# Tying the transposes and theta products of a sparse graph chunk behind the gathered products of the next chunk

## The chip, the cores and the metric

The kernel runs on one core of one Trainium2 chip. The metric is device time in microseconds (us) of one launch.

## The reference

Two graph layers with a residual and a layernorm each, on x of 8 batches, 2048 nodes, 128 features, and one adjacency matrix of 2048 x 2048 that is sparse (about 0.4% of its elements, and its diagonal, are not zero). All numbers are float32.

```python
# layer 0
res = si[:, :, None] + sj[:, None, :] + adj[None] * w_r + g_b    # si, sj: x @ parts of g_w
x = layernorm(x + einsum('bij,bjd->bid', res, x) @ weight + bias)
# layer 1: Chebyshev hops with adj, two orders (A1 and A2 are both adj)
x1 = einsum('bnf,nw->bwf', x, adj);  x2 = 2 * einsum('bnf,nw->bwf', x1, adj) - x
x = layernorm(x + relu(concat([x, x1, x2, x1, x2]) @ Theta1 + bias))
```

## The kernel before

Nodes are cut into 16 chunks of 128 rows; one row of a node holds all 8 batches (1024 numbers, 4 KB). The kernel runs in four stages.

1. To about 150 us: adj is read, masked by blocks and transposed, and each chunk is multiplied by the weight of layer 0 (Y, written to DRAM as `y0_d`). Lists of the rows that each chunk needs are made from the masks.
2. Layer 0, chunks 0 to 3, dense: all 16 blocks of a chunk are multiplied (L758).
3. Layer 0, the 12 sparse chunks, in the order of `seq`: 9 to 14, 4 to 8, 15. This is the loop that the change touches.
4. Layer 1 in two hops, `hop(1, u_d)` and `hop(2, y_d)`, over all 16 chunks. By reordering the sums, hop 1 gathers rows of `u_d`, which is the normalized x of layer 0 times a part of theta; hop 2 gathers rows of what hop 1 wrote.

A sparse chunk takes 7 gathers of 128 rows from DRAM. `gather` (L629) issues them as indirect DMAs on GpSimd (POOL) into nine buffers that are used in turn, G. All gathers of the kernel form one chain in a fixed order. Between the seven gathers of rows for a chunk, three small gathers fetch adjacency weights for later chunks into `stage` (in layer 0 and the first chunks of hop 1); `keep_r` (L657, L663, VectorE) multiplies these by a mask and puts them into `rct` (for layer 0) and `rc` (for layer 1), which hold the stationary operands.

For one sparse chunk c the loop of stage 3 issues, in program order:

- `fetch_own`, `load_x`: loads for the next chunk, on the SP queue. `put(c)`: the last of the masked weights of c.
- `own_rows` (L819): 2 products with the chunk's own rows. `listed_rows` (L837): 4 gathered blocks with 32 weight columns each, in 8 products; 2 blocks with 64 columns, in 4; 1 block with 128 columns, in 2. These 16 products are tied to each other by `in_order`.
- `make_u(*pending)`, for the chunk before c: two times `transpose4` (L182, 4 transposes each, and one copy out of PSUM, the first on VectorE at L174, the second on ScalarE at L176), then for each half 4 products with theta (L388) and a copy on ScalarE (L391), then the write of u to `u_d` on ScalarE's DMA queue (L392).
- `finish0`: two additions to x on VectorE (L371), and `layernorm`: sum (L205), mean (L208), subtraction (L209), two squares on ScalarE (L213) with their sums on VectorE (L214), square root on ScalarE (L215), reciprocal (L217), product (L218). Its result is the z that `make_u` transposes one chunk later.

After the loop, `make_u` runs once more, for chunk 15. Then hop 1 begins: `begin` for its first three chunks computes products of the transposed x with theta (L876) and with the chunk's own rows of `u_d` (L819), and the gathers from `u_d` follow, which need all of u written.

The engines' queues are not in program order: a scheduler places each instruction by the data that it needs and its own costs. Two helpers hold it: `behind` makes one instruction follow another on its engine without a semaphore, and `in_order` keeps a list of products and ties each new one behind the last. What is not tied is free to move.

```python
def in_order(mm):
    if mms:
        behind(mm, mms[-1])
    mms.append(mm)
```

Before the change, `make_u` is not tied. The scheduler puts two of the eight transposes of most chunks ahead of the products with 64 weight columns, the other six behind the last product, and the theta products between the two own-row products of the next chunk. At the end of the layer, it puts the L876 and L819 products of hop 1's first two chunks ahead of the transposes of chunk 15.

Of the kernel before, what the change touches and what calls it, by code (L numbers as in the profile page):

```python
# [18 lines left out]
def kernel(  # L19
# [29 lines left out]
    nc = tc.nc  # L49
# [4 lines left out]
    HB = B // 2  # L54
# [49 lines left out]
    def rows4(name):  # L104
        return w4.tile([P, B, D], F32, name=name, tag="w4")

    def flat(t):
        return t.rearrange("p b f -> p (b f)")


    ident = const.tile([P, P], F32)
# [59 lines left out]
    def evict(dst, src, dve=None):  # L171
        flip[0] ^= 1
        if flip[0] if dve is None else dve:
            nc.vector.tensor_copy(dst, src)  # L174
        else:
            nc.scalar.copy(dst, src)  # L176

    def transpose4(srcs, name, t=None, dve=None):

        pt = p_tr.tile([P, 4, P], F32, name=f"pt_{name}", tag="pt")  # L180
        for i, s in enumerate(srcs):
            nc.tensor.transpose(pt[:, i, :], s, ident)  # L182
        if t is None:
            t = trp.tile([P, 4, P], F32, name=f"tr_{name}", tag="tr")
        evict(t, pt, dve)
        return t
# [33 lines left out]
    def load_x(c, name, q, t=None):  # L220
        if t is None:
            t = rows4(f"{name}{c}")
        tc.keep_in_program_order(
            q.dma_start(out=t, in_=x[:, c * P:(c + 1) * P, :].rearrange("b p f -> p b f"))
        )
        return t
# [128 lines left out]
    def acc_pair():  # L355
        par[0] ^= 1
        return bank[2 * par[0]:2 * par[0] + 2]
# [9 lines left out]
    def finish0(c, accs, xr, norm=True):  # L367

        for h in range(2):
            hs = slice(h * HB, (h + 1) * HB)  # L370
            nc.vector.tensor_add(xr[:, hs, :], accs[h], xr[:, hs, :])  # L371
        if norm:
            layernorm(xr, f"0_{c}")
        return xr

    def make_u(c, z, xt, u=None):

        for h in range(2):
            transpose4([z[:, h * HB + i, :] for i in range(4)], f"p{c}_{h}",
                       xt[:, h * HB:(h + 1) * HB, :])  # L380
        if c < ND:
            nc.scalar.dma_start(out=xt_d[c], in_=flat(xt))
        if u is None:
            u = rows4(f"u{c}")
        for h in range(2):
            pp = p_sm.tile([P, HB, D], F32, name=f"pp{c}_{h}", tag="sm")
            for i in range(HB):
                nc.tensor.matmul(  # L388
                    pp[:, i, :], xt[:, h * HB + i, :], th[:, 0, :], start=True, stop=True
                )  # L390
            nc.scalar.copy(u[:, h * HB:(h + 1) * HB, :], pp)  # L391
        nc.scalar.dma_start(out=u_d[c * P:(c + 1) * P, :], in_=flat(u))  # L392

# [303 lines left out]
    def put(c):  # L697

        while jobs and jobs[0][0] == c:
            gathers(1)  # L700
        while any(w[0] == c for w in waiting):
            keep_r(*waiting.pop(0))

    pending, accs, xr = None, acc0, load_x(0, "xr", nc.sync)
    at1, ar2 = first_at[1], None
    for c in range(ND):
# [15 lines left out]
        else:  # L722
            z = finish0(c, accs, xr, c > 2)
        if c + 1 < ND:
            accs1, sit = acc_pair(), si_t(c + 1)
            at2 = first_at.get(c + 2)
            for j in range(NC):
                if c == 0:
# [7 lines left out]
                    if j == 14:  # L736
                        chunk_ranks()
                        z = finish0(c, accs, xr, False)
# [18 lines left out]
                for h in range(2):  # L757
                    mm = nc.tensor.matmul(  # L758
                        accs1[h], at1[:, j, :], Y[j][:, h * HB:(h + 1) * HB, :],
                        start=(j == 0), stop=False, skip_group_check=True,  # L760
                    )
# [4 lines left out]
        if pending is not None:  # L766
            make_u(*pending)
        z1 = z
        pending, xr = (c, z, rows4(f"xt{c}")), xr1

    def fetch(src, name, out=None):
        t = rows4(name) if out is None else out
        tc.keep_in_program_order(nc.sync.dma_start(out=flat(t), in_=src))
        return t
# [21 lines left out]
    def fetch_own(i, src, c):  # L796
        t = held.get((i, c))
        if t is None:
            t = fetch(src[c * P:(c + 1) * P, :], f"own{i}_{c}", Y[NG4 + turn[0] % 3])
            turn[0] += 1  # L800
        r = small.tile([P, P], F32, name=f"rd{i}_{c}", tag="rd", bufs=3)
        tc.keep_in_program_order(nc.sync.dma_start(
            out=r, in_=rr_d[c - ND][c * P:(c + 1) * P, 0, :] if i == 0
            else adj[c * P:(c + 1) * P, c * P:(c + 1) * P],
        ))
        own[i, c] = t, r
# [9 lines left out]
    def own_rows(i, c, accs, start):  # L816
        t, r = own.pop((i, c))
        for h in range(2):
            in_order(nc.tensor.matmul(  # L819
                accs[h], r, t[:, h * HB:(h + 1) * HB, :], start=start, stop=False,  # L820
                skip_group_check=True,
            ))
# [21 lines left out]
    with nc.allow_non_contiguous_dma(reason="512-byte rows of a diagonal block"):  # L844
        fetch_own(0, y0_d, seq[0])
        xr = load_x(seq[0], "xs", nc.sync)
        for c, c1 in zip(seq, seq[1:] + [None]):
            if c1 is not None:
                fetch_own(0, y0_d, c1)
                xr1 = load_x(c1, "xs", nc.sync)  # L850
            put(c)
            while jobs[0][0] == c1:
                gathers(1)
            accs = acc_pair()
            own_rows(0, c, accs, True)
            listed_rows(0, y0_d, c, accs)
            make_u(*pending)
            z = finish0(c, accs, xr)
            pending, xr = (c, z, x1t[c], held.get((1, c))), xr1
        for c in hops[:2]:  # L860
            fetch_own(1, u_d, c)
        for c in range(ND):
            fetch(xt_d[c], f"xt_{c}", x1t[c])
        make_u(*pending)

        def hop(i, src):
            def begin(n):
                c = hops[n]
                if (i, c) not in own:
                    fetch_own(i, src, c)  # L870
                accs = acc_pair() if n % 3 < 2 else [
                    p_sm.tile([P, HB, D], F32, name=f"acc{i}_{c}_{h}", tag="sm") for h in range(2)
                ]
                for h in range(2):
                    for b in range(HB):
                        in_order(nc.tensor.matmul(  # L876
                            accs[h][:, b, :], x1t[c][:, h * HB + b, :], th[:, i, :],
                            start=(b == 0), stop=False, skip_group_check=True,
                        ))
                own_rows(i, c, accs, False)  # L880
                return accs

            def end(c, accs):
                z = held.get((i + 1, c)) if i == 1 else None
                if z is None:
                    z = rows4(f"z{i}_{c}")
                for h in range(2):
                    hs = slice(h * HB, (h + 1) * HB)
                    if i == 1:
                        evict(z[:, hs, :], accs[h], h == 1)  # L890
                        continue
                    pt = p_tr.tile([P, HB, P], F32, name=f"pt_r{c}_{h}", tag="pt")
                    for b in range(HB):
                        in_order(nc.tensor.transpose(pt[:, b, :], x1t[c][:, h * HB + b, :], ident))  # L894
                    nc.vector.tensor_add(z[:, hs, :], accs[h], b1bc.to_broadcast([P, HB, D]))  # L895
                    nc.vector.scalar_tensor_tensor(  # L896
                        z[:, hs, :], z[:, hs, :], 0.0, pt, op0=ALU.max, op1=ALU.add
                    )
                if i == 1:
                    nc.scalar.dma_start(out=y_d[c * P:(c + 1) * P, :], in_=flat(z))  # L900
                else:
                    layernorm(z, f"1_{c}")
                    nc.scalar.dma_start(
                        out=out[:, c * P:(c + 1) * P, :].rearrange("b p f -> p b f"), in_=z
                    )

            early = [begin(n) for n in range(3)]
            for n, c in enumerate(hops):
                if i == 1 and c == 0:
                    while waiting:  # L910
                        keep_r(*waiting.pop(0))
                listed_rows(i, src, c, early[n])
                if i == 1 and n < 10:
                    gathers(3)
                if 1 <= n < NC - 2:
                    early.append(begin(n + 2))
                end(c, early[n])

        hop(1, u_d)
        hop(2, y_d)  # L920
# [21 lines left out]
    with tc.If(many == 1), nc.allow_non_contiguous_dma(reason="512-byte rows of a block"):  # L942
        for c in range(NC):
# [3 lines left out]
            z = finish0(c, accs, xr)  # L947
            nc.scalar.dma_start(out=x1_d[c * P:(c + 1) * P, :], in_=flat(z))
            make_u(c, z, rows4(f"xtd{c}"))
        for i, src in ((1, u_d), (2, y_d)):  # L950
            for c in range(NC):
                x1 = fetch(x1_d[c * P:(c + 1) * P, :], f"x1_{i}_{c}")
                xt = batches_t(x1, f"q{i}_{c}", True)
# [7 lines left out]
                z = rows4(f"zd{i}_{c}")  # L961
# [47 lines left out]
```

## Time and profile before

| | |
|---|---|
| median of 4 runs | 878.43 us (877.85 to 878.69) |
| the profiled execution | 878.73 us |
| its span, first to last instruction | 876.9 us |
| PE busy | 768.1 us (88%) |
| DVE, ACT, POOL busy | 405.8, 175.4, 437.0 us |
| TensorE clock granted, mean over the span | 0.967 |
| HBM, read and written | 345 GB/s over the span |

The profiled execution is 0.3 us above the median, and 1.8 us of it lie outside the span. In the lines of the profile, PE is TensorE's products and PEld its loads of stationary operands, DVE is VectorE, ACT is ScalarE, POOL is GpSimd, SP is SyncE; ACTq and SPq are the sequencers of these engines as they issue DMAs. A group or a line in order of time begins with its start and its length in us; the brackets at its end give the idle time of the engine ahead of it and what ended that. An idle engine is a cost only if it is the one that others wait for. float32 products with 128 moving columns appear as two passes each in the trace, products with 512 columns too, so counts of the trace are twice those of the code. Transposes appear once.

### The profile page before, as it was taken

The page shows a single profiled execution, that of the slowest core. Times are in us where ns is not written, and L with a number is a line of the kernel's source. Part 1 is how long each engine was busy: PE and PEld are TensorE (multiplying, and loading weights), DVE is VectorE, ACT ScalarE, POOL GpSimd, SP SyncE. Part 2 cuts the span into 40 slices and gives each one's busy share as a digit, 9 for nine tenths or more (in the row PEclk, how much of TensorE's full clock was granted, in tenths as well). Part 3 has the DMA queues.
Part 4 walks back from the last instruction along what each step waited for, and adds up shares of the span by engine and source line. Part 5 has one row for each costly group of instructions (what it writes and reads, how often), then busy time and mean ns, then how long its engine had stood idle before and what let it go on. Part 6 is the DMA issues. An engine that isn't in the chain of part 4 may idle for free. (4 is left out here: it accounts for less than half of the span.)

```text
span 876.9 us, 10299 instructions
## 1 busy us (share of the span) xinstructions
PE 768.1 (88%) x3607; PEld 377.1 (43%) x3607; DVE 405.8 (46%) x639; ACT 175.4 (20%) x397; POOL 437.0 (50%) x431
## 2 busy tenths in 40 slices
PE   5999999999996878979887788898999899999992
PEld 4666664465443333424335132333443334555541
DVE  5555674355984256555643000000100066677775
ACT  3655652011111112221212000000000011111111
POOL 0000000015667777777711777777653576566650
PEclk9999999899999899999989899999999999999997
DMA  8699999893386999999974899999997899999992
GB/s 281 200 311 311 300 297 294 261 364 107 79 344 183 371 344 334 345 359 367 358 306 151 283 309 333 343 326 352 372 386 278 312 321 361 341 352 358 352 351 95
DMA packets 171416, 265.05 MB, mean 302 GB/s; under 512 B 17069, under 2 KB 122069, under 8 KB 169180
## 3 DMA queue, kind: packets, MB, share of 16 engines
q0 software_dynamic: 49280, 148.61, 47.3%
q1 hardware_dynamic: 98746, 87.98, 31.1%
q10 hardware_dynamic: 23330, 27.73, 8.8%
q8 instruction: 30, 0.49, 0.2%
q14 instruction: 30, 0.25, 0.1%
HBM read 241.63 MB, written 60.96 MB: 345 GB/s over the span
## 5 line engine op out<-in xcount | busy, mean ns | idle before, releaser
L837 PE MATMUL acc<-Y,rc 128*32 128x512 f32 (+2 forms) x896 | 233.7, 611 | 36.9 <-DMA Y<-u_d,idx 30.3
L629 POOL DMA_INDIRECT Y<-y_d,idx x196 | 205.0, 1046 | 97.8 <-PE acc L837 39.5
L629 POOL DMA_INDIRECT stage<-rr_d,idx x84 | 91.5, 1089 | 229.3 <-PE acc L758 208.2
L629 POOL DMA_INDIRECT Y<-u_d,idx x112 | 111.0, 991 | 79.6 <-PE acc L819 36.9
L837 PEld LDWEIGHTS acc<-Y,rc 128*32 128x32 f32 (+2 forms) x896 | 60.5, 128 | 199.3 <-DMA Y<-u_d,idx 84.5
L837 PE MATMUL acc<-Y,rct 128*32 128x512 f32 (+2 forms) x336 | 95.9, 656 | 22.4 <-DMA Y<-y_d,idx 22.4
L758 PE MATMUL acc<-Y,wide 128*128 128x512 f32 x192 | 87.1, 603 | 0.0
L819 PE MATMUL acc<-Y,rd 128*128 128x512 f32 x140 | 67.4, 593 | 0.0
L214 DVE TENSOR_REDUCE st<-sq 128x4 f32<-128x512 f32 x64 | 43.9, 686 | 43.5 <-ACT sq L213 43.5
L174 DVE COPY z<-acc 128x512 f32<-128x512 f32 x9 | 6.2, 692 | 121.6 <-PE acc L837 74.2
L837 PEld LDWEIGHTS acc<-Y,rct 128*32 128x32 f32 (+2 forms) x336 | 23.7, 136 | 78.6 <-issue 40.2
L758 PEld LDWEIGHTS acc<-Y,wide 128*128 128x128 f32 x192 | 35.9, 194 | 39.4 <-issue 39.4
L213 ACT ACTIVATE sq<-z 128x512 f32<-128x512 f32 x32 | 20.1, 629 | 155.8 <-DVE z L209 106.0
L182 PE MATMUL pt_a<-ident,rc 128*128 128x128 f32 x240 | 35.5, 284 | 7.0 <-DMA rc<-in_adj_dram 6.5
L319 PE MATMUL acc<-wx,tr_x 128*128 128x130 f32 x256 | 36.8, 287 | 4.1 <-ACT tr_x L176 3.1
L290 DVE TENSOR_REDUCE rc<-rc 128x64 f32<-128x2048 f32 x16 | 36.5, 2280 | 7.7 <-DMA rc<-in_adj_dram 7.7
L319 PEld LDWEIGHTS acc<-wx,tr_x 128*128 128x128 f32 x256 | 32.9, 195 | 14.7 <-ACT tr_x L176 6.6
L329 PE MATMUL acc<-Y,wide 128*128 128x512 f32 x64 | 35.9, 643 | 2.5 <-ACT si L327 1.4
L371 DVE TENSOR_TENSOR xs<-acc,xs 128x512 f32<-128x512 f32 x24 | 16.6, 692 | 45.1 <-PE acc L837 45.1
L298 DVE TENSOR_REDUCE stage<-rct 128x64 f32<-128x2048 f32 x12 | 27.4, 2285 | 20.2 <-ACT rct L176 20.2
L182 PEld LDWEIGHTS pt_a<-ident,rc 128*128 128x128 f32 x240 | 29.3, 147 | 16.3 <-issue 15.0
L876 PEld LDWEIGHTS acc<-th,wide 128*128 128x128 f32 x256 | 31.0, 192 | 6.7 <-issue 6.5
(204 smaller groups left out, 884.0 us busy)
## 6 DMA issues: line engine op xcount, KB each, us to landing
rc<-in_adj_dram SPq DMA_DIRECT2D x16, 1024.0 KB
rr_d<-rct SPq DMA_DIRECT2D x12, 1024.0 KB
rr_d<-in_adj_dram SPq DMA_DIRECT2D x12, 1024.0 KB
xs<-in_x_dram SPq DMA_DIRECT2D x20, 512.0 KB
y_d<-Y SPq DMA_DIRECT2D x16, 512.0 KB
out_dram<-z ACTq DMA_DIRECT2D x16, 512.0 KB
u_d<-u ACTq DMA_DIRECT2D x14, 512.0 KB
Y<-y_d SPq DMA_DIRECT2D x14, 512.0 KB
```

The costliest lines, as they stand in the source:

```text
L182: nc.tensor.transpose(pt[:, i, :], s, ident)
L213: nc.scalar.activation(sq, z[:, hs, :], AF.Square)
L214: nc.vector.tensor_reduce(st[:, 2, hs], sq, AX.X, ALU.add)
L290: nc.vector.tensor_reduce(mk[:, c, :], a.rearrange("p (w f) -> p w f", f=TW), AX.X, ALU.max, apply_absolute_value=True,)
L298: nc.vector.tensor_reduce(mkt[:, :, 4 * c:4 * c + 4], at.rearrange("p j (t f) -> p j t f", f=TW), AX.X, ALU.max, apply_absolute_value=True,)
L319: nc.tensor.matmul(py[:, i, 0:D + 2], xt[b // HB][:, (b + i) % HB, :], wx, start=True, stop=True,)
L329: nc.tensor.matmul(acc0[h], first_at[0][:, c, :], Y[c][:, h * HB:(h + 1) * HB, :], start=(c == 0), stop=False, skip_group_check=True,)
L629: g = nc.gpsimd.indirect_dma_start(out=out, out_offset=None, in_=src, in_offset=bass.IndirectOffsetOnAxis(ap=ids[:, n:n + 1], axis=0), bou ...
L758: mm = nc.tensor.matmul(accs1[h], at1[:, j, :], Y[j][:, h * HB:(h + 1) * HB, :], start=(j == 0), stop=False, skip_group_check=True,)
L819: in_order(nc.tensor.matmul(accs[h], r, t[:, h * HB:(h + 1) * HB, :], start=start, stop=False, skip_group_check=True,))
L837: in_order(nc.tensor.matmul(accs[h][w * t:w * t + w], r[:, o + w * t:o + w * t + w], gs[t][:, h * HB * D:(h + 1) * HB * D], start=False, s ...
L876: in_order(nc.tensor.matmul(accs[h][:, b, :], x1t[c][:, h * HB + b, :], th[:, i, :], start=(b == 0), stop=False, skip_group_check=True,))
```

## The change

`make_u` and `transpose4` get an argument `tie`, a function that is called with each transpose and each theta product. In the loop over the sparse chunks and after it, `in_order` is passed. So the transposes and the theta products of the chunk before stand in one fixed chain with the own-row and gathered products: own rows of c, the 14 gathered products of c, 8 transposes and 8 theta products of the chunk before c, own rows of the next chunk, and so on. After the loop, transposes and theta products of chunk 15 follow those of chunk 8, and only then the first products of hop 1. The calls of `make_u` in the dense chunks and in the fallback path pass no `tie` and stay as they were. No instruction is added or removed, and the order on the queues of SP and POOL is the same.

```diff
-    def transpose4(srcs, name, t=None, dve=None):
+    def transpose4(srcs, name, t=None, dve=None, tie=None):
         pt = p_tr.tile([P, 4, P], F32, name=f"pt_{name}", tag="pt")
         for i, s in enumerate(srcs):
-            nc.tensor.transpose(pt[:, i, :], s, ident)
+            mm = nc.tensor.transpose(pt[:, i, :], s, ident)
+            if tie is not None:
+                tie(mm)
...
-    def make_u(c, z, xt, u=None):
+    def make_u(c, z, xt, u=None, tie=None):
         for h in range(2):
             transpose4([z[:, h * HB + i, :] for i in range(4)], f"p{c}_{h}",
-                       xt[:, h * HB:(h + 1) * HB, :])
+                       xt[:, h * HB:(h + 1) * HB, :], tie=tie)
...
             for i in range(HB):
-                nc.tensor.matmul(
+                mm = nc.tensor.matmul(
                     pp[:, i, :], xt[:, h * HB + i, :], th[:, 0, :], start=True, stop=True
                 )
+                if tie is not None:
+                    tie(mm)
...
             listed_rows(0, y0_d, c, accs)
-            make_u(*pending)
+            make_u(*pending, tie=in_order)
...
             fetch(xt_d[c], f"xt_{c}", x1t[c])
-        make_u(*pending)
+        make_u(*pending, tie=in_order)
```

## The prediction

> **What bounds the kernel now.** The change touches only the sparse chunks of layer 0, 284 to 478 us of the 876.9 us span, so I read that stretch first by windows (length, busy time and count of PE, PEld, DVE, ACT, POOL; then granted clock, DMA share, GB/s), then by waits, then one chunk in order of time.
>
> ```profile
> 284.00:441.50 157.50, 132.12 (x598) 55.66 (x599) 83.62 (x141) 32.99 (x61) 122.22 (x110) 0.94 0.98 355
> 441.50:455.00 13.50, 9.84 (x51) 4.24 (x50) 7.46 (x14) 3.22 (x6) 0.00 (x0) 0.93 0.97 386
> 455.00:478.00 23.00, 21.82 (x116) 14.35 (x112) 8.00 (x11) 4.97 (x9) 0.00 (x0) 0.89 0.31 109
> ```
>
> POOL issues 110 gathers in 157.5 us, 1.43 us each; the DMA engines are 0.98 busy. The waits of PE and POOL there (total, times, longest):
>
> ```profile
> PE acc L837 <- DMA Y<-y_d,idx: 22.4, 13, 10.1
> PE pt_p L182 <- DVE xs L218: 13.3, 8, 3.1
> ...
> POOL Y L629 <- issue: 13.7, 45, 0.3
> POOL Y L629 <- PE acc L837: 7.5, 18, 1.8
> ```
>
> PE loses 13.3 us in front of transposes that stand before their layernorm is done. But POOL hardly waits for PE: its gaps are 0.3 us, the distance between any two gathers, but for two (0.75 and 1.84). It issues without pause, so a stall of PE is paid for only if it delays a gather. One chunk in order of time:
>
> ```profile
> 401.57 1.23 DVE L209 TENSOR_TENSOR xs<-xs,st 128x1024 f32<-128x1024 f32 x1
> 402.20 1.48 POOL L629 DMA_INDIRECT stage<-rr_d,idx  x1 [0.30 <-DMA Y<-y_d,idx]
> 402.42 0.58 ACT L391 COPY u<-pp 128x512 f32<-128x512 f32 x1 [0.31 <-PE pp L388]
> 402.90 0.63 ACT L213 ACTIVATE sq<-xs 128x512 f32<-128x512 f32 x1
> 403.03 0.33 ACTq L392 DMA_DIRECT2D u_d<-u  x1
> 406.24 1.22 DVE L218 TENSOR_TENSOR xs<-xs,rs 128x1024 f32<-128x1024 f32 x1
> 406.59 1.74 POOL L629 DMA_INDIRECT Y<-y_d,idx  x1 [0.30 <-issue]
> 407.58 0.28 DVE L663 TENSOR_SCALAR rct<-stage,has 128x128 f32<-128x128 f32 x1
> 407.61 0.41 PE L182 MATMUL pt_p<-ident,xs 128*128 128x128 f32 x2 [2.07 <-DVE xs L218]
> 407.95 0.64 PE L837 MATMUL acc<-Y,rct 128*64 128x512 f32 x1
> ```
>
> Two things decide. First, a gather takes 0.99 us, but one that starts while L209 or L218 runs ends 0.87 us after it (406.24 + 1.22 + 0.87 = 408.33 = 406.59 + 1.74); one that starts just before is not stretched. Second, the 64-row products behind the stalled transposes wait themselves for the masked weights that DVE writes at L663, after L218.
>
> **What the Trainium skill says.** "SBUF — State Buffer", Who interferes with whom: a DVE instruction with two SBUF inputs contends with a GpSimd instruction that reads SBUF, and whoever starts first has the port. L209 and L218 have two such inputs and a gather reads its list there; the trace agrees (1.48 and 1.74 us against 0.99), though the same section adds that tensor_tensor did not stall DMAs, which this trace contradicts. "TensorE: Matmul & The Clock Gate", Part 1: after an idle window of some 3.4 us TensorE runs at half clock until a busy one has passed. The trace agrees: idle 477.25 to 483.28, then a clock of 0.50 from 480.5 to 487.3. Same page, Architectural detail: ScalarE's queue is strictly in order; nothing in the trace contradicts it (the write at 403.03 follows the copy that it waits for).
>
> **The change, part by part.** Nothing is added or removed: PE's 8 transposes and 8 theta products (16 passes in the trace) of each of 13 chunks (the last dense one, then the 12 sparse ones) get a fixed place. The order of the built instructions shows what moves. SP's and POOL's queues keep their order.
>
> *1. Transposes behind the products.* Before, two (of 8) stand ahead of the 64-row products, 6 behind. The 13.3 us of stalls disappear from the transposes and come back in front of the 64-row products, which need L663: after the stall they started at 407.95, 0.37 us after L663 began. Gain for PE: nothing. Cost: two transposes more at the end of a chunk, 2 x 0.11 = 0.22 us (pitch from 6 in 0.82 us), hidden: theta waits for the copies, which still start as DVE is through with its two L371.
>
> *2. Own rows behind theta.* The L819 products that filled the wait for the copies (443.15 - 442.34 = 0.8 us) come after theta, so the next 32-row products start up to 0.9 us later. Cover: they then wait for their gathers, or PE for L663, anyway. Zero.
>
> *3. ACT.* In ten of the twelve chunks the write of u (L392) now stands ahead of the first square (L213) of the next layernorm. It waits for the second copy (402.42 + 0.58 = 403.00) and takes 0.33 us, so the square starts at 403.4 and not 402.90: L218 comes 0.5 us later, 5.15 us after L209 and not 4.66. Queued behind: layernorm, L663, the 64-row products. The loop from a chunk's last product (E) to the next chunk's is E+9.2 to the 64-row products and 3.7 for those and the last two: 12.9 us now (398.75 to 407.95), 13.4 then. Chunks are 14.0 us apart ((441.5 - 315.7) / 9), so the loop keeps 0.6 us of room.
>
> *4. POOL.* After a stretched L209 gather, gathers start at L209 + 2.40, 3.70, 4.99, 6.29. L218 at 4.66 caught the one at 4.99 (wait 0.33 to 0.40, stretch 0.7). At 5.15 it starts 0.16 us after that one, and the next, at 6.29, is free of it (6.29 + 0.99 = 7.28 against 5.15 + 1.22 + 0.87 = 7.24). In all 19 of these gathers are stretched, by 12.8 us together; the eight L218 ones of the chunks 11 to 14 and 4 to 7 make 5.9 of it. If they go, POOL needs 13.3 to 13.5 us a chunk. I take less: the loop of 13.4 us and a DMA share that rises from 0.98 towards 1.0 let through about a quarter of 5.9, **-1.5 us** (ends -5 and 0).
>
> *5. The end of the layer.* Now the begin products of hop 1 (L876, L819) fill PE while the last layernorm runs, and the transposes of chunk 15 stand behind them:
>
> ```profile
> 468.16 1.22 DVE L218 TENSOR_TENSOR xs<-xs,rs 128x1024 f32<-128x1024 f32 x1
> ...
> 470.20 1.04 PE L182 MATMUL pt_p<-ident,xs 128*128 128x128 f32 x8
> ...
> 474.35 0.33 ACTq L392 DMA_DIRECT2D u_d<-rc  x1
> ...
> 478.03 0.99 POOL L629 DMA_INDIRECT Y<-u_d,idx  x1 [36.56 <-PE acc L819]
> ```
>
> Then make_u of 8 and of 15 stand together, with PE idle from about 464.0 to 469.8 (L218's end 469.4, plus 0.4 by part 3). The transposes start 0.4 us earlier, but at half clock, as 6.0 us of idle time gave at 483: 8 transposes in 1.8 us for 0.9, theta up to 3.7 for 1.9. Fully slow, the write of u goes out 1.5 us later; full speed, 0.4 earlier. I take **+0.6** (a window that ends between). The first gather of hop 1 moves by as much, because it waits for that write. The begin products, 3 x 3.5 = 10.5 us, end near 485.5, 1.6 us after the first gather lands (483.3 + 0.6); two 512 KB loads of own rows, issued at 466.9 and 470.4 before, now fall into hop 1's first gathers (1 MB at 350 GB/s, 3 us of DMA). Both are covered: POOL issues hop 1's gathers without pause to 616 us with the DMA at 0.92. From 478 on all shifts by the +0.6.
>
> Sum: -1.5 + 0.6 = -0.9 us on the profiled execution's 878.73, 877.8; its median stands 0.3 lower: **877.5 us**.
>
> **Rivals.**
> *A slower layer 0.* If L218 lands before the gather and not after it (0.16 us of margin), the stretch becomes up to 1.1 us in place of 0.7: +0.4 x 8 = 3.2; and each slow-clock window in the loop (three 3.4 us windows now, 309.8, 378.0 and 408.8; each costs 1.5 to 2.1 us: 12 products in 5.98 for 3.85 at 408) uses up its 0.6 us of room. It decides from 0.4 us of shift downwards, or from one more such window in three chunks. With half of the first, one more window and +0.6: 1.6 + 1.8 + 0.6 = +4.0, **882.4 us**. For it: the margin is small. Against: in the trace no L209 or L218 starts in the first 0.1 us of a gather, and all that start 0.1 us or more after it leave it alone.
> *PE's stalls are real time.* If the 13.3 us were on the path, 866 us. Against: L663, and POOL's missing waits. I give it only the tail.
> *It does nothing.* The DMA at 0.98 sets the stage, and the end's two effects cancel: **878.4 us**.
>
> **How the numbers follow.** This kernel's measurement tells 0.2% (1.8 us) from no change. The first case 0.53, whose own range is -4.5 to +1.5 (parts 4 and 5 at their ends): faster 0.28, same 0.22, slower 0.03. The slower rival 0.32: slower 0.29, same 0.03. Nothing 0.13: same 0.11, slower 0.02. Stalls real 0.02. Together faster 0.30, same 0.36, slower 0.34. The range, 873.8 to 882.6, runs from the first case's lower end to the slower rival.
>
> **What would show it.** Right: the wait of L182 for L218 gone, PE waiting as long before L837 for L663; L209 to L218 5.1 us; gathers over 1.4 us about half as many; an idle PE from 464 to 469 and then a clock near 0.5; the first gather of u_d within 1 us of where it was relative to the last product. Wrong: stretched gathers as many as now or longer, or chunks under 13.3 us apart (PE's stalls did count), or over 14.3 (the loop binds).

## The result, and the profile after

| | before | after |
|---|---|---|
| median, in runs of the two side by side | 878.15 us (63 runs) | 882.08 us (42 runs) |
| ratio after to before, 95% interval | | 1.0036 (1.0025 to 1.0046) |
| profiled execution | 878.73 us | 879.59 us |
| its span | 876.9 us | 877.7 us |

The change costs 0.36%, about 3 us; the ratios in this document compare the fast runs of two kernels, so they can stand up to 0.2% off the ratio of the two medians (here 1.0045, or 3.9 us). The profiled execution of after is 2.5 us faster than its median, so part of the loss is not in its trace; single executions of either kernel spread over 9 to 11 us. Where a difference is small I therefore go by many runs, and read from traces only what several of them show.

First the windows, with the columns of the prediction (length, busy time and count of PE, PEld, DVE, ACT, POOL, clock, DMA share, GB/s):

```profile
284.00:441.50 157.50, 127.13 (x628) 59.85 (x632) 86.73 (x146) 35.38 (x64) 112.80 (x111) 0.97 1.00 362
441.50:455.00 13.50, 5.14 (x24) 1.03 (x16) 3.60 (x8) 1.56 (x3) 0.00 (x0) 0.69 0.82 297
455.00:478.00 23.00, 16.59 (x93) 12.83 (x92) 7.99 (x11) 5.07 (x9) 1.23 (x2) 0.81 0.18 65
```

The loop did get faster: POOL needs 112.8 us there, where it needed 122.2, and the DMA share rises from 0.98 to 1.00. But in the next 13.5 us PE does 5.1 us of work (9.8 before) at a clock of 0.69: part of what was won is lost right behind the loop. The groups of the page and the waits (total, times, longest) say what became of the gathers (first before, then after) and of PE's stalls (after):

```profile
L629 POOL DMA_INDIRECT Y<-y_d,idx x196 | 205.0, 1046 | 97.8 <-PE acc L837 39.5
L629 POOL DMA_INDIRECT stage<-rr_d,idx x84 | 91.5, 1089 | 229.3 <-PE acc L758 208.2
```

```profile
L633 POOL DMA_INDIRECT Y<-y_d,idx x196 | 198.0, 1010 | 104.8 <-issue 47.6
L633 POOL DMA_INDIRECT stage<-rr_d,idx x84 | 88.5, 1053 | 229.7 <-DMA y_d<-Y 187.9
```

```profile
PE acc L841 <- DVE rct L661: 25.3, 10, 8.4
...
PE acc L841 <- DMA Y<-y_d,idx: 12.9, 6, 9.4
...
ACT sq L215 <- DMA Y<-u_d: 6.5, 1, 6.5
```

Line numbers after are up to 4 higher than before (L209 is now L211, L218 is L220, L371 is L373). The two groups of gathers are 7.0 and 3.0 us shorter than before. PE's wait of the transposes for the layernorm is gone, and PE waits for the masked weights in its place. The last line is new: a square waits 6.5 us, once, for a load of `u_d` rows that it does not read. One chunk of the loop in order of time:

```profile
411.04 1.23 DVE L211 TENSOR_TENSOR xs<-xs,st 128x1024 f32<-128x1024 f32 x1
...
411.88 0.58 ACT L395 COPY u<-pp 128x512 f32<-128x512 f32 x1 [0.31 <-PE pp L390]
...
412.50 0.33 ACTq L396 DMA_DIRECT2D u_d<-u  x1
412.87 0.63 ACT L215 ACTIVATE sq<-xs 128x512 f32<-128x512 f32 x1 [0.40 <-ACT u L395]
...
416.10 1.00 POOL L633 DMA_INDIRECT Y<-y_d,idx  x1 [0.30 <-DMA Y<-y_d,idx]
416.21 1.23 DVE L220 TENSOR_TENSOR xs<-xs,rs 128x1024 f32<-128x1024 f32 x1
417.35 0.28 DVE L661 TENSOR_TENSOR rct<-stage,has 128x128 f32<-128x128 f32 x1
417.41 1.09 POOL L633 DMA_INDIRECT Y<-y_d,idx  x1 [0.30 <-issue]
...
417.69 2.23 PE L841 MATMUL acc<-Y,rct 128*64 128x512 f32 x8 [1.48 <-DVE rct L661]
```

The write of u (412.50) is ahead of the square; L220 starts 5.17 us after L211, 0.11 us after one gather, and the next one is 1.09 us long, not 1.7. The same queue at the end of the loop, where chunk 8 is finished and the write is that of chunk 7, first before, then after:

```profile
425.40 0.57 SPq L773 DMA_DIRECT2D Y<-u_d  x1
...
445.69 0.63 ACT L213 ACTIVATE sq<-xs 128x512 f32<-128x512 f32 x1
445.83 0.33 ACTq L392 DMA_DIRECT2D u_d<-u  x1
...
454.00 6.75 PE L837 MATMUL acc<-Y,rct 128*64 128x512 f32 x10 [2.18 <-DMA Y<-y_d,idx]
```

```profile
421.17 11.37 SPq L777 DMA_DIRECT2D Y<-u_d  x1
...
439.54 0.58 ACT L395 COPY u<-pp 128x512 f32<-128x512 f32 x1 [0.31 <-PE pp L390]
...
446.25 0.33 ACTq L396 DMA_DIRECT2D u_d<-u  x1
446.62 0.63 ACT L215 ACTIVATE sq<-xs 128x512 f32<-128x512 f32 x1 [6.50 <-DMA Y<-u_d]
...
449.96 1.22 DVE L220 TENSOR_TENSOR xs<-xs,rs 128x1024 f32<-128x1024 f32 x1
...
451.44 6.48 PE L841 MATMUL acc<-Y,rct 128*64 128x512 f32 x12 [8.36 <-DVE rct L661]
```

The copy is done at 440.12, the write goes out at 446.25. In the trace's operands this write signals the completion of its transfer on semaphore 108, and so does the load of own rows that SP began to issue at 421.17; the last packet of that load counted at 446.17. Eight such semaphores are used in turn by the loads and writes of SP and ScalarE, so a transfer waits for the one eight places before it: in the other three profiles with this wait (below) the write also goes out 0.07 to 0.08 us after the last count of the load. In the kernel before, the same write also used 108, but there its predecessor was the write of chunk 6, done at 439.0. In the changed order chunk 6's write stands ahead of the load and no longer behind it, so the load has 108. The load itself came late; SP needed 11.37 us to issue it, 0.57 before. Behind the stuck write stand the squares, L220 and the masked weights of chunk 15, and PE, having waited 8.4 us, runs its last 12 passes (6 products) at half clock in 6.48 us. Half clock alone is not new there: in the kernel before, PE waits at this place for the last gathered rows, and its last ten passes run at half clock as well (the clock record has 0.5 from 453.2 to 460.0; the prediction lists three slow windows in the loop and misses this one). Last, the end of the layer, theta before and then all of it after:

```profile
471.68 2.02 PE L388 MATMUL pp<-th,Y 128*128 128x128 f32 x16 [0.44 <-DVE Y L174]
```

```profile
465.83 1.22 DVE L220 TENSOR_TENSOR xs<-xs,rs 128x1024 f32<-128x1024 f32 x1
...
467.20 1.94 PE L182 MATMUL pt_p<-ident,xs 128*128 128x128 f32 x8 [5.79 <-DVE xs L220]
...
469.17 2.67 PE L390 MATMUL pp<-th,Y 128*128 128x128 f32 x16
...
472.49 0.33 ACTq L396 DMA_DIRECT2D u_d<-rc  x1
...
476.47 0.99 POOL L633 DMA_INDIRECT Y<-u_d,idx  x1 [39.96 <-issue]
```

Both groups of PE are longer than before (1.94 for 1.04, 2.67 for 2.02), after 5.8 us without work. In the table, a "y gather" is one of the layer's own gathers, and its end is that of GpSimd's instruction; the rows land later. "E" below is the end of the last sparse product, read as the start of the first L373 of chunk 15.

| | last y gather ends | E | first gather of hop 1 | end of span |
|---|---|---|---|---|
| before | 441.47 | 459.72 | 478.03 | 876.9 |
| after | 436.51 | 457.10 | 476.47 | 877.7 |

Of 5.0 us won in the gathers, 2.6 are left at E and 1.6 at the first gather of hop 1. From there to the end the profiled execution loses 2.4 us; in the profiles below this stretch takes 399 to 402 us with and without the tie at the end, so I don't count it to the change.

### The profile page after: what moved, and what is told of

Read it like the earlier page. It is cut to its first block, busy times and chain, and to the rows that moved or that the text cites. A ratio compares the mean times of both kernels' runs of the same rounds, so it can differ in the third digit from the quotient of the medians.

```text
span 877.7 us, 10280 instructions
## 1 busy us (share of the span) xinstructions
PE 758.6 (86%) x3607; PEld 379.9 (43%) x3607; DVE 405.2 (46%) x639; ACT 176.3 (20%) x397; POOL 426.8 (49%) x431
## 4 chain that ended last, share of the span: by engine, by line
PE 45%; DMA 26%; issue 12%; DVE 7%; ACT 5%; POOL 3%; POOLq 0%; SPq 0%; ACTq 0%; DVEq 0%
PE acc L841 15%; DMA Y<-u_d,idx 11%; DMA Y<-y_d,idx 8%; PE acc L762 6%; PE acc L331 4%; PE acc L321 4%; PE acc L880 3%; PE acc L823 3%; DMA xs<-in_x_dram 3%; PE pp L390 3%; POOL Y L633 2%; PE pt_a L182 2%; DMA u_d<-u 1%; DVE st L216 1%; ACT sq L215 1%
## 5 line engine op out<-in xcount | busy, mean ns | idle before, releaser
L633 POOL DMA_INDIRECT Y<-y_d,idx x196 | 198.0, 1010 | 104.8 <-issue 47.6
L633 POOL DMA_INDIRECT stage<-rr_d,idx x84 | 88.5, 1053 | 229.7 <-DMA y_d<-Y 187.9
L841 PE MATMUL acc<-Y,rct 128*32 128x512 f32 (+2 forms) x336 | 83.6, 625 | 38.4 <-DVE rct L661 25.3
L174 DVE COPY z<-acc 128x512 f32<-128x512 f32 x9 | 6.2, 692 | 122.2 <-PE acc L841 74.4
L215 ACT ACTIVATE sq<-z 128x512 f32<-128x512 f32 x32 | 20.1, 629 | 158.1 <-DVE z L211 131.9
L373 DVE TENSOR_TENSOR xs<-acc,xs 128x512 f32<-128x512 f32 x24 | 16.6, 692 | 54.1 <-PE acc L841 54.1
```

What stands on the lines that cost most here:

```text
L215: nc.scalar.activation(sq, z[:, hs, :], AF.Square)
L633: g = nc.gpsimd.indirect_dma_start(out=out, out_offset=None, in_=src, in_offset=bass.IndirectOffsetOnAxis(ap=ids[:, n:n + 1], axis=0), bou ...
L841: in_order(nc.tensor.matmul(accs[h][w * t:w * t + w], r[:, o + w * t:o + w * t + w], gs[t][:, h * HB * D:(h + 1) * HB * D], start=False, s ...
```

## The experiments

Ratios are to the kernel before, run beside each on the same chip; its median was 877.6 to 878.9 us there, except on the two chips named below.

**The changed kernel again.**

> The changed kernel once more, as it is, for a second profile of it. In the first profile of it the write of u of the last chunk but one stood 6.1 us in ScalarE's queue (440.1 to 446.2 us) with the first square of the last sparse chunk's layernorm behind it, until a load of own rows had landed. Theory W (the stuck write): the same wait is there again, 3 to 9 us long, and the time is 881 to 883 us. Theory E (the end of the layer: transposes and theta of the last chunk behind hop 1's first products, at half clock): the wait may be there or not, the time is 881 to 883 us all the same, and PE idles about 5 us ahead of the last transposes. Theory D (nothing but a different phase of hops and clock windows): neither is there twice, time 880 to 883 us.

Measured: 880.47 us, 1.0023 (1.0009 to 1.0038). The write of chunk 7 was stuck again, for 4.8 us, and from E to the first gather of hop 1 it took 20.7 us (18.3 before). (The expectation names the chunks one too late: the write is chunk 7's, and the layernorm behind it is that of chunk 8, the last but one.) Theory D falls; W and E are both left.

**Each tie alone.** The first kernel ties in the loop only, and was run twice (the second time as `e8_loop_only_b`); the other ties only the last `make_u`.

```diff
-        make_u(*pending, tie=in_order)     # after the loop: tie in the loop only
+        make_u(*pending)
```

```diff
-            make_u(*pending, tie=in_order) # in the loop: tie at the end only
+            make_u(*pending)
```

> The changed kernel with the tie taken off the last make_u alone (the one after the loop), so that the last sparse chunk's transposes and theta stand where the scheduler puts them. Theory W: 881 to 883 us, as the changed kernel, because the write is still ahead of the square. Theory E: 876.5 to 878 us, because the end is that of the kernel before and the loop's shorter gathers stay. Theory D: 880 to 883 us.

> The tie in the loop alone once more, on another occasion, since its gain was near the uncertainty. If the loop's tie saves what the shorter gathers give (1.5 us): 0.1 to 0.25% under the kernel before. If the first time was chance: within 0.1% of it or above.

> The tie on the last make_u alone; the loop as in the kernel before. Theory W: 878 to 879 us, as the kernel before plus the 0.6 us that the prediction gave the end. Theory E: 881 to 883 us, all of the loss. Theory D: 877 to 879 us.

Measured: tie in the loop 0.9990 (0.9976 to 1.0005) and 0.9992 (0.9973 to 1.0011); tie at the end 1.0034 (1.0013 to 1.0056). On the one chip on which all three ran, the medians are 880.47 us with both ties, 877.29 with the tie in the loop and 880.56 with the tie at the end. So the tie at the end is enough for the whole loss, as theory E has it; the tie in the loop gives perhaps 0.8 us, and neither run alone tells that from nothing. In the second profile of the loop's tie the write of chunk 7 was stuck for 5.7 us, and E came at 454.9. In the first it was not, and E came at 452.9: there SP issued the load in 0.91 us, and it landed at 442.2, before the write was ready.

**TensorE kept busy at the end.** 42 transposes of the identity, never read, go in front of the last `make_u`: first in the changed kernel, then with the tie at the end alone.

```diff
+        pk = p_tr.tile([P, 4, P], F32, name="pk", tag="pt")
+        for k in range(42):
+            in_order(nc.tensor.transpose(pk[:, k % 4, :], ident, ident))
         make_u(*pending, tie=in_order)
```

> The changed kernel with 42 extra transposes of the identity (result never used) between theta of the last chunk but one and the transposes of the last chunk, so that TensorE is busy in the 5 to 6 us in which it waits for the last layernorm. Theory clock (the end loses by half clock): the last transposes and theta run at full speed, the last write of u comes 14.6 to 14.8 us after the last sparse product and not 15.4 to 16.5, and the time is 0.8 to 1.8 us under the changed kernel's, 879 to 881 us. Theory order (the end loses because hop 1's first products and own rows stand behind, whatever the clock): within 0.5 us of the changed kernel, 880.5 to 882.5 us.

> The tie on the last make_u alone, with the 42 extra transposes in front of it that keep TensorE busy while it waits for the last layernorm. If half clock is the whole loss of the end: the last write of u comes 14.3 to 14.6 us after the last sparse product, the first gather of hop 1 about 18 us after it (20.05 without the extra work), and the time goes from 1.003 of the kernel before to 0.999 to 1.001. If the place of hop 1's first products and own rows costs too: the gather at 18 us all the same, but hop 1 takes longer and the time stays at 1.002 to 1.004.

> The tie on the last make_u alone with the 42 extra transposes, again, since on the chip of the first try every kernel took 4% longer and the interval was too wide. Half clock is the whole loss of the end: 0.999 to 1.001 of the kernel before, first gather of hop 1 about 18 us after the last sparse product. The place of hop 1's first products costs too: 1.002 to 1.004.

Measured: changed kernel with the extra work 877.32 us, 0.9994 (0.9978 to 1.0010), where the changed kernel has 1.0023 and 1.0036; tie at the end with it 1.0005 (0.9988 to 1.0021), where it has 1.0034. The first try of the latter fell on a chip on which every kernel, the one before included, took 4% longer (912 us); it gave 1.0007 (0.9973 to 1.0040), which tells nothing. The end of the layer in the third of these kernels, in order of time:

```profile
463.99 4.53 PE L870 MATMUL pk<-ident 128*128 128x128 f32 x40
...
468.07 1.22 DVE L220 TENSOR_TENSOR xs<-xs,rs 128x1024 f32<-128x1024 f32 x1
469.35 1.09 PE L182 MATMUL pt_p<-ident,xs 128*128 128x128 f32 x8 [0.83 <-DVE xs L220]
470.88 2.02 PE L390 MATMUL pp<-th,Y 128*128 128x128 f32 x16 [0.44 <-DVE Y L174]
473.56 0.33 ACTq L396 DMA_DIRECT2D u_d<-rc  x1
477.58 0.99 POOL L633 DMA_INDIRECT Y<-u_d,idx  x1 [34.61 <-issue]
```

Transposes and theta take 1.09 and 2.02 us. From E (here 459.78), in the profiles from chips of the usual speed:

| | to the last write of u | to the first gather of hop 1 |
|---|---|---|
| before | 14.6 | 18.3 |
| tie in the loop (two profiles) | 15.3, 15.3 | 18.7, 18.7 |
| both ties (two profiles) | 15.4, 16.5 | 19.4, 20.7 |
| tie at the end | 15.8 | 20.1 |
| both ties, extra work | 14.3 | 18.0 |
| tie at the end, extra work | 13.8 | 17.8 |

The extra work leaves the order of the other products at the end as the tie has it, and 0.29% came back both times (0.20% and 0.12% by the plain medians). For each pair the two intervals still touch at their ends; the one with extra work in the changed kernel is apart from that of the first result (1.0025 to 1.0046). On one chip the changed kernel with the extra work (877.32 us) stood level with the tie in the loop alone (877.53 us). Together with the traces this makes the loss of the tie at the end half clock, not the place of hop 1's first products.

**The write behind the square root.** In the changed kernel, then with the tie in the loop alone, each write of u is issued behind L217 of the next layernorm.

```diff
-            make_u(*pending, tie=in_order)
-            z = finish0(c, accs, xr)
+            write = make_u(*pending, tie=in_order, late=True)   # late: returns the write
+            z = finish0(c, accs, xr, write=write)
...
+        root = nc.scalar.activation(st[:, 3], st[:, 2], AF.Sqrt, bias=epst, scale=1.0 / D)
+        if write is not None:
+            behind(write(), root)
```

> The changed kernel with one more edit: in the loop the write of u is issued behind the square root of the next layernorm, so that no square, reduction or masked weight stands behind it. Theory W: the last layernorm starts on time, the last sparse products come up to 6 us earlier and partly at full clock; 874 to 878 us, at or below the kernel before. Theory E: 881 to 883 us, unchanged. Theory D: 880 to 883 us.

> The tie in the loop alone, and the write of u behind the square root of the next layernorm. If the write's place in ScalarE's queue costs the loop time (0.5 us a chunk ahead of the square, 6 us when it is stuck): 875 to 876.5 us, 1 to 2 us under the tie in the loop alone. If it costs nothing, because transfers set the stage: 877 to 878 us, as the tie in the loop alone.

Measured: 0.9997 (0.9979 to 1.0015) and 0.9976 (0.9959 to 0.9992). The first, 878.23 us, speaks for theory W (874 to 878) and against theory E (881 to 883): late writes too bring the changed kernel back to level, with the tie at the end still in it and 19.3 us from E to the first gather of hop 1. Their gain is 0.26% on the changed kernel and 0.16% on the tie in the loop, each run on the same chip, with intervals that overlap. The stuck write is gone, but so is the loop's own gain: L220 is back at 4.7 us after L211, 20 and 18 gathers are over 1.2 us long (8 and 12 in the two profiles of the changed kernel, 18 before), and chunks are 14.3 us apart for 13.8 and 13.9. The half microsecond of part 3 is what frees the gathers. But these kernels are not slower for their longer gathers, so what the freed gathers are worth in time is not shown.

**Only chunk 7's write behind the square root.** This keeps that half microsecond and frees the one write that was stuck. The edit is shown against the kernel with all writes late.

```diff
-            write = make_u(*pending, tie=in_order, late=True)
+            write = make_u(*pending, tie=in_order, late=c == seq[-2])
```

> The tie in the loop alone, and of the writes of u only that of chunk 7 (made while the last chunk but one is finished, the one that was stuck for 5 to 6 us in four profiles) put behind the next square root. If the stuck write is what the late writes save: the last sparse product comes 15 us or less after the end of the last y gather (19 to 21 where it was stuck), and the time is 0.997 to 0.998, as with all writes late. If the half microsecond per chunk is what they save: as the tie in the loop alone, 0.999.

> The tie in the loop alone with only the write of u of chunk 7 put behind the square root, again for the same reason. Stuck write: 0.997 to 0.998, last sparse product 15 us or less after the last y gather. Half a microsecond per chunk: 0.999.

Measured, with the tie in the loop alone: 1.0003 (0.9979 to 1.0027) on the chip of 912 us; then 871.25 us, 0.9918 (0.9888 to 0.9949), in six runs of 868.8 to 872.8 us on a chip where the kernel before took 874.0 to 883.0. That is the fastest version of all, beyond both marks above, though from six runs on one chip. Its chunk 8 in order of time:

```profile
443.38 0.59 ACT L397 COPY u<-pp 128x512 f32<-128x512 f32 x1 [0.31 <-PE pp L392]
443.86 0.63 ACT L215 ACTIVATE sq<-xs 128x512 f32<-128x512 f32 x1
...
448.68 1.94 PE L845 MATMUL acc<-Y,rct 128*64 128x512 f32 x8 [1.76 <-DVE rct L665]
...
448.92 0.33 ACTq L399 DMA_DIRECT2D u_d<-u  x1
...
450.95 1.95 PE L845 MATMUL acc<-Y,rct 128*128 128x512 f32 x4 [0.34 <-DMA Y<-y_d,idx]
452.09 0.69 DVE L375 TENSOR_TENSOR xs<-acc,xs 128x512 f32<-128x512 f32 x1 [2.87 <-PE acc L845]
```

The write still waits, to 448.92, but nothing of the layernorm stands behind it; the last 12 passes take 3.9 us at full clock, and E is 452.1, 11.6 us after the last y gather (18.2 before, 20.6 in the changed kernel). The same one move in the changed kernel, without and with the extra transposes:

> The changed kernel, both ties in place, with the write of u of chunk 7 alone put behind the next square root. If the stuck write is the main loss: 0.994 to 0.996 of the kernel before (the 0.992 of the same move with the end untied, and 0.003 for the tied end), and the last sparse product within 15 us of the last y gather. If that 0.992 was chance: 1.000 to 1.003.

> The same with the 42 extra transposes in front of the last make_u. If the two costs add: 0.990 to 0.993. If half clock costs nothing once the write is free: as the same kernel without the extra transposes, 0.994 to 0.996. If the move of chunk 7's write was chance: 0.998 to 1.000.

Both met a chip of 912 us again: 1.0025 (0.9994 to 1.0055) and 1.0002 (0.9969 to 1.0036). By the marks set above, the first falls to "chance" and the second lies next to it. On the slower chips POOL waits for 53 to 63 us in the loop (36 in the kernel before), and the DMA share in it is 0.90 to 0.97; the kernels that this move was made in were not run there without it, so what freeing the write gives on them is not known. That the gain of 0.8% holds on other chips of the usual speed was not shown.

**Both repairs, with all writes late.**

> The changed kernel with both repairs: the write of u behind the square root, and the extra transposes in front of the last make_u. If the two costs are separate and add up (2 to 3 us for the clock, 1 to 2 us for the write): 0.996 to 0.998 of the kernel before. If one of them was the same time seen twice: 0.999 to 1.000.

> The changed kernel with late writes and extra transposes, again for the same reason. The costs are separate: 0.996 to 0.998. The same time seen twice: 0.999 to 1.000.

Measured: 0.9979 (0.9945 to 1.0013) on a slower chip, 0.9991 (0.9970 to 1.0011) on a usual one: not told from no change, nor from the changed kernel with either repair alone. Each repair alone brings the changed kernel back to level, and whether the two add is open.

**Masked weights ahead of the layernorm.** Tie in the loop alone, next chunk's `keep_r` ahead of the layernorm on DVE; then with late writes too.

```diff
-            z = finish0(c, accs, xr)
+            if c1 is not None:
+                put(c1)
+            z = finish0(c, accs, xr, pin=kept[0] if c1 is not None else None)  # kept: the last masked weight
```

> The tie in the loop alone, and the next chunk's masked weights put ahead of the layernorm on VectorE, so that no product waits for a layernorm. If transfers set the stage (DMA share 0.98 to 1.00 there): TensorE's wait of about 25 us for the masked weights goes and comes back as waits for gathers, pitch of chunks 13.5 to 14.0 us, 876 to 878.5 us. If TensorE's stalls are time on the path: pitch under 13.3 us and 866 to 873 us.

> The tie in the loop alone, masked weights of the next chunk ahead of the layernorm, and all writes of u behind the square root. If transfers set the stage: no better than the late writes alone, 0.997 to 0.998. If waits of TensorE still count where gathers do not cover them: 0.993 to 0.996.

> The tie in the loop alone, early masked weights and late writes, again for the same reason. Transfers set the stage: 0.997 to 0.998. Waits of TensorE count too: 0.993 to 0.996 (0.9955 was measured on the slower chip, where gathers were slower).

Measured: 0.9981 (0.9961 to 1.0002); with late writes 0.9955 (0.9928 to 0.9983) on a slower chip and 0.9991 (0.9974 to 1.0007) on a usual one. PE's longest waits in the loop of the first:

```profile
PE acc L844 <- DMA Y<-y_d,idx: 25.3, 21, 10.0
PE pp L390 <- DVE wide L174: 4.8, 8, 0.6
```

No product waits for the masked weights any more, and PE waits 25.3 us for gathers instead; POOL needs 122 us as in the kernel before (113 to 118 with the tie in the loop). So on chips of the usual speed PE's waits for the masked weights are not time that can be had this way: the forecast of 866 to 873 us, for stalls that count, did not come. As the gathers grew longer in the same step, the two effects are not told apart.

## Why the prediction was wrong

It named 877.5 us, with a small gain as its likeliest case (0.53), and by outcome 0.30 for faster, 0.36 for the same and 0.34 for slower; the change loses 3 us. 882.08 lies in the range, near the 882.4 of the slower rival, but not by that rival's mechanism: that the numbers are close is chance.

- **Part 1 held.** The 13.3 us of the transposes' wait became part of 25.3 us of waits for masked weights in front of the 64-row products, 8.4 of it the stuck write; the waits for gathers fell from 22.4 to 12.9. The early masks agree that these waits, the stuck write's apart, are not on the path.
- **Part 2 held**: in the chunk shown, the 32-row products start 6.0 us after E and not 5.1 (413.50 and 403.17), as forecast, and PE still has 1.48 us to wait for the masked weights behind them.
- **Part 3 was right in the half microsecond and wrong in what it is worth.** L220 came 5.17 us after L211 (5.15 forecast). But the write was priced at its 0.33 us of issue and never at a wait of its own. That chunk 6's write moved ahead of a load of own rows, so that chunk 7's came to share a semaphore with that load, could be read from the built order; the prediction did not look at what the writes wait for. Chunk 7's write was stuck in four of the five profiles taken on chips of the usual speed that have the loop's tie and neither late writes nor early masks (4.8 and 6.1 us in the changed kernel's two). ScalarE's strict order, which the prediction took from the Trainium skill ("TensorE: Matmul & The Clock Gate", Architectural detail), is what makes it matter, and this trace shows it at 446.25 and 446.62.
- **Part 4 had the right mechanism.** POOL saved 10.0 us of gather time over the kernel, more than the 5.9 counted on. The 1.5 us for the time is 0.8 as measured by the loop's tie alone (0.9990 and 0.9992), and neither interval leaves out no change. The DMA share went to 1.00, SP's loads came later, and one of them held the write. That the faster gathers pushed the loads back is likely, but was not tried: in the first profile of the loop's tie the share is 1.00 too, and no single issue of SP in the loop took over 2.9 us.
- **Part 5 is the term that failed**: the price of the end was too low. The idle stretch from 464 to 470 and the half clock were forecast where they came (461.4 to 467.2, clock 0.5 from 463.7 to 470.5). The Trainium skill ("TensorE: Matmul & The Clock Gate", Part 1) says that the clock halves after an idle window of some 3.4 us and comes back after a busy one, and the trace agrees in the main: 5.79 us without work, and 0.5 in them and behind them; here the clock halves 2.3 us after PE's last work (461.4 to 463.7), sooner than after a whole such window. But the term stood at +0.6, ends -0.4 and +1.5, for a window that ends between. From E to the last write it was 15.4, 16.5 and 15.8 us in the three profiles with the tie at the end, for 14.6: +1.3 on the mean. From the write to the first gather it was 4.0 to 4.3 us, for 3.7, which the prediction didn't have at all: +0.5 (the write's transfer landed up to 0.3 us later, and POOL started 0.2 to 0.3 later after that; why was not tried). Together +1.7 us in the traces, where the tie in the loop alone has +0.4. By the ratio of the tie at the end it is +3.0 (1.0034, with an interval from 1.1 to 4.9; the plain medians give 1.6), of which 2.5 come back with the extra transposes (0.0029 of 878 us, both times).

The sum as it came out: -0.8 for the loop and +3.0 for the end is +2.2, beside measured +2.0 (1.0023) and +3.2 (1.0036). The rest of up to 1 us is within the intervals. So the sum was wrong by the end's +3.0 for +0.6, and in the second place by the loop's -0.8 for -1.5. The slower rival's mechanism, L218 ahead of the gather, did not happen: L220 started 0.11 us after one. "Stalls are real" had 866 us, and falls with the result and with the early masks (876.5). "It does nothing" falls with the interval.

What stays open: how much the stuck write costs. Where it is stuck, E comes 2 us later than where it is not (454.9 and 452.9, tie in the loop alone). Its repair was worth 0.7% in the one comparison on a chip of the usual speed, which is 6 us and more than these traces account for: E came at 452.1 with the repair, 0.8 us ahead of the profile without it in which the write was not stuck. Late writes brought the changed kernel back to level without touching its end; why that is as much as the end costs is not explained either.

## What to carry to other kernels

When an order is fixed by hand, look at what each moved instruction's neighbours wait for, DMAs on in-order compute queues above all: a write that was free can inherit a completion semaphore from a late load, and everything behind it stops. Price an idle stretch of TensorE by what runs right after it; if that work is on the path to the next stage, some otherwise useless products in the gap may be cheaper than the half clock. And when a stage's DMA share is near 1, ask of every faster gather which other transfer now comes late.

## What the runs showed of the hardware that I had not expected

- SP's issue of a 512 KB load of rows, 0.57 us in the kernel before, took 11.37 us in the changed kernel (421.17), and three other loads there took 7.5 to 13.1 us, at a DMA share of 1.00 in the loop; the loads behind it on the queue went out later too. A share of 1.00 is not enough for it: with the tie in the loop alone, the first profile has 0.91 us for the same load.
- Half a microsecond in the start of one VectorE product decides over the length of GpSimd's gathers: with L220 at 5.2 us after L211, 8 and 12 gathers were over 1.2 us long (the changed kernel); at 4.7 us it was 17 to 20 (the kernels with all writes late, on chips of the usual speed).
- On two of the chips the kernel before took 912 and not 878 us; the kernels profiled there had a DMA share of 0.90 to 0.97 in the loop, so a price in microseconds from one chip need not hold on another.
